# Merging the small TensorE products of two units in a Mamba block on Trainium2

## The chip, the cores and the metric

The kernel runs on one core of one Trainium2 chip. What is measured is the device time of one launch in microseconds (us). The core has five engines that run side by side and wait for each other through semaphores: TensorE (PE, with its weight loads shown apart as PEld), VectorE (DVE), ScalarE (ACT), GpSimd (POOL) and SyncE (SP, which here issues nearly all transfers).

## The reference

The block has four sequences of 512 tokens with 512 features. A conditioning vector gives six modulation vectors. The input is normalised, scaled and shifted, sent through a Mamba-2 layer, gated and added back; then it is normalised again, sent through a linear layer with a binarised weight, gated and added back. Cut to the Mamba layer, which is what the change touches:

```python
xBCzA = einsum('bld,ed->ble', h, in_proj_w)          # x, B, C, z and one step size per head
xBC   = silu(conv1d_4(xBC) + bias)                   # x: 64 heads of 16; B, C: 8 groups of 64
dt    = softplus(A_log)                              # (b, l, 64)
A_cum = cumsum(-dt) inside chunks of 128 tokens
Y_diag = (C . B) * exp(segsum(A)) applied to x       # inside a chunk
states = B^T . (x * exp(A_cum[-1] - A_cum))          # what a chunk leaves behind
new_states: states carried from chunk to chunk, decayed by exp(A_cum[-1])
Y_off  = (C . states) * exp(A_cum)                   # what earlier chunks add
out    = einsum((Y_diag + Y_off + D * x / dt) * silu(z + z_bias), out_proj_w)
```

All arrays are float32.

## The kernel before, in words

The 2048 tokens are eight halves `h` of 256 tokens, two to a sequence. Each half has two chunks `c` of 128 tokens, and the eight B/C groups are taken two at a time, as four pairs `gp`. A unit is one `(h, c, gp)`: 16 heads in one chunk. There are 64 units, and the loop at the end (lines 822 to 840) takes one unit a step. Feature rows stand on the 128 partitions, the two groups of a pair in the two halves of the partitions.

At step `s` of that loop the program first records the work of the next half (projections and convolutions for x, B, C and z in `conv_pair` and `f_z`, normalisation, step sizes in `f_dt`, transposes), spread over the steps by the lists `FRONT`, `FIRST` and `SECOND`, and the tails of finished chunks (output projection `tail1`, line 716; normalisation; linear layer `tail3`, line 753). Then it records the unit's own work:

- `burst(old, new)` (lines 593 to 607): the two products of unit `s` with the carried states (`gy<-C,S`, none in the first chunk of a sequence) and the two products B times C of unit `s+2` (`gy<-C,B`). Each product takes half of the partitions as its rows, so the two of a pair run side by side in the array (shown as `64*128`). They land in one PSUM tile `gy`, which has a single buffer of two banks and four slots of 128 columns; slots 0 and 1 are used.
- `stage2` of unit `s` (lines 627 to 694): 16 products `py` in two groups of eight (`128*32`, four side by side); DVE adds them to the state part (lines 663, 668) and POOL adds the skip and multiplies with the gate (669, 672). For the state that the chunk leaves, POOL makes `xd` (line 679, two buffers), PE the two products `pst` (line 684, `128*64`, side by side), and DVE copies them (687) or adds them to the decayed old state that POOL has made (689, 694). The states of a chunk are one tile `S` of four pairs.
- `stage0` and `stage1` of unit `s+2`: the loads of the running sums, the exponentials on ACT (line 544, 16 for a unit), the masked `gm` out of `gy` (618), and two large multiplications on DVE (622). `gm` and the unit's `yt` share three buffers.

`f_dt` (line 353) forms the product of the step sizes, `pa`, with eight matmuls of 64 columns (line 366), over k and, inside, over the two chunks; their right side is `hT`, which ACT writes one k at a time (line 347).

`glued` (line 208) keeps a list of matmuls together: the later ones are tied to the first and get a high priority. Lines 210 and 213 are its own, so `gy` and `py` show these two lines. Otherwise the order on each engine is set by a scheduler that takes the recorded instructions and their dependencies; matmuls that are not glued may be parted by others, as those of `pa` and `pst` are in some places. [...] The accumulators of the projections and the `pa` and `pst` tiles share five PSUM buffers (`mm`).

Of the kernel before, what the change touches and what calls it, by code (L numbers as in the profile page):

```python
# [11 lines left out]
F32 = mybir.dt.float32  # L12
# [4 lines left out]
P = 128  # L17
# [22 lines left out]
def adaln_mamba_block(  # L40
# [18 lines left out]
    def bc(ap, n):  # L59

        return ap.unsqueeze(2).to_broadcast([ap.shape[0], ap.shape[1], n])

    def bc_mid(ap, n):

        return ap.unsqueeze(1).to_broadcast([ap.shape[0], n, ap.shape[1]])
# [287 lines left out]
    def f_dt(h):  # L353

        hT = H[h]["hT"]

        def small(tag, bufs=1):  # L360
            return wk.tile([P, CH], F32, tag=tag, name=f"{tag}_{h}", bufs=bufs)

        pa = ps.tile([P, CH], F32, tag="mm", name=f"pa_{h}")
        for k in range(NK):
            for c in range(2):
                mm(pa[c * NH : (c + 1) * NH, :], win[:, k, NCONV + DI :],
                   hT[:, k, KS - 1 + c * CH : KS - 1 + (c + 1) * CH], start=(k == 0), stop=(k == NK - 1))
        u, r, q, dt, relu = (small(n) for n in ("du", "dr", "dq", "da", "dl"))
        nc.vector.tensor_scalar(relu, pa, 0.0, None, ALU.max)
        nc.scalar.activation(u, pa, AF.Abs)  # L370
        nc.scalar.activation(u, u, AF.Exp, scale=-1.0)
        nc.vector.tensor_scalar(r, u, 2.0, None, ALU.add)
        nc.vector.reciprocal(r, r)
        nc.vector.tensor_mul(u, u, r)
        nc.vector.tensor_mul(q, u, u)
        nc.vector.tensor_scalar(dt, q, SERIES[0], None, ALU.mult)
        for cf in SERIES[1:]:
            nc.vector.scalar_tensor_tensor(dt, dt, cf, q, ALU.add, ALU.mult)
        nc.vector.scalar_tensor_tensor(dt, dt, 1.0, u, ALU.add, ALU.mult)
# [12 lines left out]

        ntot = wk.tile([P, 1], F32, tag="ntot", name=f"ntot_{h}", bufs=1)
        nc.vector.tensor_scalar(ntot, up[:, CH - 1 : CH], -1.0, None, ALU.mult)
        ed = u
        nc.scalar.activation(ed, up, AF.Exp, bias=ntot)

        dg = q
        nc.vector.tensor_scalar(dg, ident, es[:, CH - 1 : CH], None, ALU.mult)

        nc.vector.reciprocal(r, dt)
        nc.vector.tensor_scalar(r, r, dsk, None, ALU.mult)
        with tc.issue_after(last_win):
            for c in range(2):
                nc.sync.dma_start(r_d[h, :, c, :], r[c * NH : (c + 1) * NH, :])
        H[h].update(turn=(sh, ed, dg))
# [185 lines left out]

    def burst(old, new):

        gy = ps.tile([P, 2, 4, CH], F32, tag="gy", bufs=1, name="gy_" + "_".join(map(str, old or new)))
        products = []
        if old is not None:
            h, c, gp = old
            k = (h % HPB) * 2 + c
            if k > 0:  # L600
                products += by_rows(gy, 1, h, c, gp, states[h // HPB, k][:, gp, :])
                G[old, 1] = gy
        if new is not None:
            h, c, gp = new
            products += by_rows(gy, 0, h, c, gp, H[h]["B"][gp // 2][:, gp % 2, c * CH : (c + 1) * CH])
            G[new, 0] = gy
        glued(products)

    def stage1(h, c, gp):

        n = f"{h}_{c}_{gp}"
        ets, e = U0.pop((h, c, gp))
        gm = wk.tile([P, 2, CH], F32, tag="gm", name=f"gm_{n}", bufs=3)
        nc.vector.tensor_mul(gm, G.pop(((h, c, gp), 0))[:, :, 0, :], bc_mid(upto, 2))  # L618
        if (h, c, gp) not in AHEAD:
            exps(h, c, gp, ets)  # L620
        for r in range(2):
            nc.vector.scalar_tensor_tensor(  # L622
                ets[r], ets[r], 1.0, bc_mid(gm[:, r, :], HPG), ALU.min, ALU.mult
            )
        U1[h, c, gp] = (ets, e)

    def stage2(h, c, gp):

        n = f"{h}_{c}_{gp}"
        k = (h % HPB) * 2 + c
# [12 lines left out]
        for r in range(2):  # L646
            glued([
                partial(
                    mm, py[32 * j : 32 * j + 32, r, :],
                    xp[:, r * 2 * P + 32 * (2 * j + q) : r * 2 * P + 32 * (2 * j + q) + 32],  # L650
                    ets[r][:, 2 * j + q, :], start=(q == 0), stop=(q == 1),
                )
                for q in range(2) for j in range(HPG // 2)
            ])

        cs = slice(c * CH, (c + 1) * CH)
        zg = H[h]["z"][gp][:, :, cs]
        xs = H[h]["xs"][gp][:, :, cs]
        t = wk.tile([P, 2, CH], F32, tag="gm", name=f"yt_{n}", bufs=3)

        ew = nc.vector if h == NHALF - 1 and c == 1 and gp >= NP // 2 else nc.gpsimd
        if k > 0:
            nc.vector.tensor_mul(t, G.pop(((h, c, gp), 1))[:, :, 1, :], e)
            if ew is nc.vector:
                ew.tensor_add(t, t, xs)
                ew.tensor_add(t, py, t)
            else:
                nc.vector.tensor_add(t, py, t)  # L668
                ew.tensor_add(t, t, xs)  # L669
        else:  # L670
            nc.vector.tensor_add(t, py, xs)  # L671
        ew.tensor_mul(zg, t, zg)  # L672

        if k < HPB * 2 - 1:
            if gp == 0:
                states[b, k + 1] = wk.tile([P, NP, P], F32, tag="S", name=f"S_{b}_{k + 1}")
            new = states[b, k + 1][:, gp, :]
            xd = wk.tile([P, HPG, 2, HD], F32, tag="xd", name=f"xd_{n}")
            nc.gpsimd.tensor_tensor(xd, xg, by_head(H[h]["ed"][:, hd0 : hd0 + HPP]), ALU.mult)  # L679
            xd2 = xd.rearrange("p j q e -> p (j q e)")  # L680
            pst = ps.tile([P, P], F32, tag="mm", name=f"pst_{n}")
            bt = H[h]["bt"][gp // 2][:, c, gp % 2, :]
            for r in range(2):
                mm(pst[r * NS : (r + 1) * NS, :], bt[:, r * NS : (r + 1) * NS], xd2[:, r * P : (r + 1) * P],  # L684
                   start=True, stop=True)
            if k == 0:
                nc.vector.tensor_copy(new, pst)
            else:
                nc.gpsimd.tensor_tensor(
                    new.rearrange("p (h e) -> p h e", e=HD),  # L690
                    states[b, k][:, gp, :].rearrange("p (h e) -> p h e", e=HD),
                    bc(H[h]["dec"][:, c * NP + gp, :], HD), ALU.mult,
                )
                nc.vector.tensor_add(new, new, pst)


    gates = {}
# [124 lines left out]
    for step in range(-1, max(steps) + 1):  # L822
        for f, args in steps.get(step, []):
            f(*args)

        new = units[step + 2 : step + 3] if step >= 0 else units[0:2]
        if step < 0:
            for unit in new:
                burst(None, unit)
                stage0(*unit)  # L830
                stage1(*unit)
        elif step < len(units):
            if new or not is_first(*units[step][:2]):
                burst(units[step], new[0] if new else None)
            stage2(*units[step])
            for unit in POST.get(step, []):
                ahead(*unit)
            for unit in new:
                stage0(*unit)
                stage1(*unit)  # L840
# [42 lines left out]
```

## Time and profile before

| | |
|---|---|
| median of 3 runs | 755.07 us (753.83 to 756.47) |
| the profiled execution | 755.08 us, of which the span of instructions is 753.4 us |
| mean granted TensorE clock | 0.984 |
| busy: PE, PEld | 713.0 us (95%), 505.6 us (67%) |
| busy: DVE, ACT, POOL | 610.8 us (81%), 520.1 us (69%), 258.5 us (34%) |
| instructions of line 684 (`pst`) and 366 (`pa`) as recorded passes | 192 and 128 |
| passes of `gy`: with B, with S | 256 and 192 |

A float32 matmul shows as two records (passes) in the trace, so that four records are one pair of products lying side by side. "Busy" of PE is modelled from start times; the start times themselves are recorded, and the time of a group of matmuls is best read from its own start to the start of the next group. Idle time of an engine that does not set the pace costs nothing.

### The profile page before, as it was taken

Reading aid. Unit: us, or ns where it says so; the run is one execution under the profiler, and the core shown is the slowest. Engines: PE = TensorE matmul, PEld = TensorE weight load, DVE = VectorE, ACT = ScalarE, POOL = GpSimd, SP = SyncE. Lnnn points to the kernel's source line nnn. Section 1 sums busy time; section 2 is a strip of 40 time slices with the busy share of each in tenths; the row PEclk is TensorE's granted clock in tenths of the full one; section 3 lists DMA queues with packets and bytes.
Section 4 is the critical chain, followed back from the end, with each engine's and each line's share of the span. In section 5 each row is a group of like instructions: output and inputs, shape, how many; then the busy total and the mean of one; then the engine's idle time right before and its main releaser. Section 6 shows DMA issues by size and latency. Waiting matters only on the chain. (4 is left out here: it accounts for less than half of the span.)

```text
span 753.4 us, 15095 instructions
## 1 busy us (share of the span) xinstructions
PE 713.0 (95%) x5196; PEld 505.6 (67%) x5196; DVE 610.8 (81%) x1226; ACT 520.1 (69%) x1503; POOL 258.5 (34%) x293
## 2 busy tenths in 40 slices
PE   6999868999999999999999999999999999999977
PEld 3786646766678666767677666786666766776643
DVE  3869888876998689976999669986898849996983
ACT  2486557749696587776777596875868758798920
POOL 4022345443143322343242341353213332334540
PEclk9999979999999999999999999999999999999989
DMA  8991583636553363424563355343634337455710
GB/s 282 313 291 42 188 193 96 166 80 144 117 142 105 84 173 105 130 68 112 142 154 105 75 142 136 113 127 90 163 89 111 93 84 182 123 161 124 161 35 28
DMA packets 121308, 99.25 MB, mean 132 GB/s; under 512 B 73984, under 2 KB 99840, under 8 KB 121232
## 3 DMA queue, kind: packets, MB, share of 16 engines
q1 hardware_dynamic: 120944, 97.76, 49.8%
q8 instruction: 41, 0.67, 0.4%
q10 hardware_dynamic: 288, 0.52, 0.2%
q14 instruction: 35, 0.29, 0.1%
HBM read 92.47 MB, written 5.79 MB: 130 GB/s over the span
## 5 line engine op out<-in xcount | busy, mean ns | idle before, releaser
L544 ACT ACTIVATE decay<-decay,st 128x128 f32<-128x128 f32 x960 | 293.3, 396 | 13.5 <-DMA decay<-sums_d 13.2
L622 DVE SCALAR_TENSOR_TENSOR decay<-decay,gm 128x1024 f32<-128x1024 f32 x120 | 155.3, 1295 | 28.3 <-ACT decay L544 26.4
L432 PE MATMUL pp_x<-hT,win 128*128 128x259 f32 x512 | 119.7, 388 | 0.0
L432 PE MATMUL pp_z<-hT,win 128*128 128x256 f32 x512 | 118.1, 383 | 0.0
L716 PE MATMUL po<-wout,z 128*128 128x512 f32 x256 | 114.2, 598 | 0.0
L679 POOL TENSOR_TENSOR xd<-xpad,st 128x256 f32<-128x256 f32 x48 | 35.0, 729 | 212.5 <-PE pst L684 161.1
L432 PEld LDWEIGHTS pp_x<-hT,win 128*128 128x128 f32 x512 | 96.2, 192 | 17.3 <-issue 2.6
L432 PEld LDWEIGHTS pp_z<-hT,win 128*128 128x128 f32 x512 | 94.3, 189 | 16.1 <-issue 3.0
L669 POOL TENSOR_TENSOR yt<-yt,xs 128x256 f32<-128x256 f32 x46 | 43.7, 950 | 128.5 <-DVE yt L668 115.9
L716 PEld LDWEIGHTS po<-wout,z 128*128 128x128 f32 x256 | 47.9, 191 | 53.8 <-issue 53.2
L449 DVE SCALAR_TENSOR_TENSOR u_x<-pp_x,cw,u_x 128x256 f32<-128x256 f32 x192 | 82.7, 474 | 0.8 <-ACT u_x L445 0.3
L213 PE MATMUL py<-decay,xpad 128*32 128x128 f32 x1680 | 68.8, 280 | 0.0
L511 ACT ACTIVATE uz<-pp_z,zb 128x256 f32<-128x256 f32 x64 | 26.8, 468 | 58.3 <-PE pp_z L432 58.3
L432 PE MATMUL pp_B<-hT,win 128*128 128x259 f32 x256 | 62.2, 395 | 0.8 <-DVE u_x L449 0.7
L672 POOL TENSOR_TENSOR z<-yt,z 128x256 f32<-128x256 f32 x62 | 57.2, 922 | 11.6 <-DVE yt L671 8.2
L502 POOL TENSOR_TENSOR xs<-u_x,rr 128x512 f32<-128x512 f32 x32 | 44.1, 1378 | 46.4 <-DVE u_x L454 38.4
L753 PE MATMUL pf<-bwT,h 128*128 128x512 f32 (+1 forms) x136 | 59.3, 576 | 0.6 <-ACT h L737 0.6
L432 PE MATMUL pp_C<-hT,win 128*128 128x259 f32 x256 | 59.5, 385 | 0.0
L445 ACT ACTIVATE u_x<-pp_x,cb,cw 128x256 f32<-128x256 f32 x64 | 35.1, 559 | 33.1 <-PE pp_x L432 32.9
L210 PE MATMUL py<-decay,xpad 128*32 128x128 f32 x240 | 48.0, 282 | 8.5 <-ACT decay L544 6.8
L432 PEld LDWEIGHTS pp_B<-hT,win 128*128 128x128 f32 x256 | 48.1, 194 | 11.2 <-DVE u_x L449 1.5
L432 PEld LDWEIGHTS pp_C<-hT,win 128*128 128x128 f32 x256 | 48.4, 192 | 7.8 <-issue 0.5
(155 smaller groups left out, 1144.5 us busy)
## 6 DMA issues: line engine op xcount, KB each, us to landing
decay<-sums_d SPq DMA_DIRECT2D x120, 256.0 KB
decay<-sums_d SPq DMA_DIRECT2D x120, 128.0 KB
rr<-r_d SPq DMA_DIRECT2D x64, 128.0 KB
e<-e_d SPq DMA_DIRECT2D x96, 64.0 KB
win<-in_w_inT SPq DMA_DIRECT2D x4, 1024.0 KB
xr<-in_x SPq DMA_DIRECT2D x16, 256.0 KB
res<-o SPq DMA_DIRECT2D x15, 256.0 KB
x<-in_x SPq DMA_DIRECT2D x14, 256.0 KB
```

What stands on the lines that cost most here:

```text
L210: first = products[0]()
L213: product()
L432: last = mm(pm, win[:, k, col : col + P], H[h]["hT"][:, k, lo:], start=(k == 0), stop=(k == NK - 1))
L445: nc.scalar.activation(u[:, j, :], pm[:, KS - 1 :], AF.Identity, bias=cb[:, t : t + 1], scale=cw[:, t, KS - 1 : KS])
L449: nc.vector.scalar_tensor_tensor(u[:, j, :], pm[:, k : k + T], cw[:, t, k : k + 1], u[:, j, :], ALU.mult, ALU.add)
L502: nc.gpsimd.tensor_tensor(xs, xc, rr, ALU.mult)
L544: nc.scalar.activation(ets[r][:, i, :], ets[r][:, i, :], AF.Exp, bias=H[h]["st"][:, hd : hd + 1], scale=-1.0)
L622: nc.vector.scalar_tensor_tensor(ets[r], ets[r], 1.0, bc_mid(gm[:, r, :], HPG), ALU.min, ALU.mult)
L669: ew.tensor_add(t, t, xs)
L672: ew.tensor_mul(zg, t, zg)
L716: last_po = mm(po, H[h]["z"][g // 2][:, g % 2, c * CH : (c + 1) * CH], wout[:, g, :], start=(g == 0), stop=(g == NKI - 1))
L753: mm(pf, h2[:, k, :], bwT[:, k, cols], start=(k == 0), stop=(k == NK - 1))
```

## The change

Three things are done in larger pieces. A burst now serves two units at once: at every even step it forms the state products of units `s` and `s+1` and the B times C products of units `s+2` and `s+3`, in all four slots of `gy`; at odd steps there is none. The new states of two neighbouring pairs are formed together at the odd step, by a new function: four glued products into one PSUM tile, and one copy, or one multiplication and one addition, of 256 columns. The product of the step sizes is glued, and takes k downwards in every half but the first.

```diff
@@ f_dt
-        for k in range(NK):
-            for c in range(2):
-                mm(pa[c * NH : (c + 1) * NH, :], win[:, k, NCONV + DI :],
-                   hT[:, k, KS - 1 + c * CH : KS - 1 + (c + 1) * CH], start=(k == 0), stop=(k == NK - 1))
+        ks = range(NK) if h == 0 else range(NK - 1, -1, -1)
+        glued([
+            partial(
+                mm, pa[c * NH : (c + 1) * NH, :], win[:, k, NCONV + DI :],
+                hT[:, k, KS - 1 + c * CH : KS - 1 + (c + 1) * CH], start=(k == ks[0]), stop=(k == ks[-1]),
+            )
+            for k in ks for c in range(2)
+        ])
@@ burst
-        if old is not None:
-            h, c, gp = old
+        for i, (h, c, gp) in enumerate(old):
             k = (h % HPB) * 2 + c
             if k > 0:
-                products += by_rows(gy, 1, h, c, gp, states[h // HPB, k][:, gp, :])
-                G[old, 1] = gy
-        if new is not None:
-            h, c, gp = new
-            products += by_rows(gy, 0, h, c, gp, H[h]["B"][gp // 2][:, gp % 2, c * CH : (c + 1) * CH])
-            G[new, 0] = gy
+                products += by_rows(gy, 2 + i, h, c, gp, states[h // HPB, k][:, gp, :])
+                G[(h, c, gp), 1] = gy[:, :, 2 + i, :]
+        for i, (h, c, gp) in enumerate(new):
+            products += by_rows(gy, i, h, c, gp, H[h]["B"][gp // 2][:, gp % 2, c * CH : (c + 1) * CH])
+            G[(h, c, gp), 0] = gy[:, :, i, :]
         glued(products)
@@ stage2
-            if gp == 0:
-                states[b, k + 1] = wk.tile([P, NP, P], F32, tag="S", name=f"S_{b}_{k + 1}")
-            new = states[b, k + 1][:, gp, :]
             xd = wk.tile([P, HPG, 2, HD], F32, tag="xd", name=f"xd_{n}")
             nc.gpsimd.tensor_tensor(xd, xg, by_head(H[h]["ed"][:, hd0 : hd0 + HPP]), ALU.mult)
-            ...
+            XD[gp % 2] = xd.rearrange("p j q e -> p (j q e)")
+            if gp % 2:
+                new_states(h, c, gp - 1)
+
+    XD = {}
+
+    def new_states(h, c, gp):
+        k = (h % HPB) * 2 + c
+        b = h // HPB
+        if gp == 0:
+            states[b, k + 1] = wk.tile([P, NP, P], F32, tag="S", name=f"S_{b}_{k + 1}")
+        both = slice(gp, gp + 2)
+        new = states[b, k + 1][:, both, :].rearrange("p g e -> p (g e)")
+        pst = ps.tile([P, 2, P], F32, tag="mm", name=f"pst_{h}_{c}_{gp}")
+        bt = H[h]["bt"][gp // 2]
+        glued([
+            partial(
+                mm, pst[r * NS : (r + 1) * NS, i, :], bt[:, c, i, r * NS : (r + 1) * NS],
+                XD[i][:, r * P : (r + 1) * P], start=True, stop=True,
+            )
+            for i in (1, 0) for r in range(2)
+        ])
+        pst = pst.rearrange("p g e -> p (g e)")
+        if k == 0:
+            nc.vector.tensor_copy(new, pst)
+        else:
+            nc.gpsimd.tensor_tensor(
+                new.rearrange("p (h e) -> p h e", e=HD),
+                states[b, k][:, both, :].rearrange("p g (h e) -> p (g h) e", e=HD),
+                bc(H[h]["dec"][:, c * NP + gp : c * NP + gp + 2, :].rearrange("p j h -> p (j h)"), HD), ALU.mult,
+            )
+            nc.vector.tensor_add(new, new, pst)
@@ the loop over steps
         if step < 0:
+            burst([], new)
             for unit in new:
-                burst(None, unit)
                 stage0(*unit)
                 stage1(*unit)
         elif step < len(units):
-            if new or not is_first(*units[step][:2]):
-                burst(units[step], new[0] if new else None)
+            if step % 2 == 0 and (step + 2 < len(units) or not is_first(*units[step][:2])):
+                burst(units[step : step + 2], units[step + 2 : step + 4])
             stage2(*units[step])
```

More of the change, by code (lines that the diff above doesn't have):

```diff
@@ L593, in burst @@
     def burst(old, new):
-        gy = ps.tile([P, 2, 4, CH], F32, tag="gy", bufs=1, name="gy_" + "_".join(map(str, old or new)))
+        gy = ps.tile([P, 2, 4, CH], F32, tag="gy", bufs=1, name="gy_" + "_".join(map(str, (old or new)[0])))
         products = []
-        if old is not None:
-            h, c, gp = old
+        for i, (h, c, gp) in enumerate(old):
             k = (h % HPB) * 2 + c
             if k > 0:
-                products += by_rows(gy, 1, h, c, gp, states[h // HPB, k][:, gp, :])
-                G[old, 1] = gy
-        if new is not None:
-            h, c, gp = new
-            products += by_rows(gy, 0, h, c, gp, H[h]["B"][gp // 2][:, gp % 2, c * CH : (c + 1) * CH])
-            G[new, 0] = gy
+                products += by_rows(gy, 2 + i, h, c, gp, states[h // HPB, k][:, gp, :])
[3 more added lines that the diff above has]
+            G[(h, c, gp), 0] = gy[:, :, i, :]
         glued(products)
@@ L617, in stage1 @@
         gm = wk.tile([P, 2, CH], F32, tag="gm", name=f"gm_{n}", bufs=3)
-        nc.vector.tensor_mul(gm, G.pop(((h, c, gp), 0))[:, :, 0, :], bc_mid(upto, 2))
+        nc.vector.tensor_mul(gm, G.pop(((h, c, gp), 0)), bc_mid(upto, 2))
         if (h, c, gp) not in AHEAD:
@@ L662, in stage2 @@
         if k > 0:
-            nc.vector.tensor_mul(t, G.pop(((h, c, gp), 1))[:, :, 1, :], e)
+            nc.vector.tensor_mul(t, G.pop(((h, c, gp), 1)), e)
             if ew is nc.vector:
@@ L674, in stage2 @@
         if k < HPB * 2 - 1:
-            if gp == 0:
-                states[b, k + 1] = wk.tile([P, NP, P], F32, tag="S", name=f"S_{b}_{k + 1}")
-            new = states[b, k + 1][:, gp, :]
             xd = wk.tile([P, HPG, 2, HD], F32, tag="xd", name=f"xd_{n}")
             nc.gpsimd.tensor_tensor(xd, xg, by_head(H[h]["ed"][:, hd0 : hd0 + HPP]), ALU.mult)
-            xd2 = xd.rearrange("p j q e -> p (j q e)")
-            pst = ps.tile([P, P], F32, tag="mm", name=f"pst_{n}")
-            bt = H[h]["bt"][gp // 2][:, c, gp % 2, :]
@@ L683, in stage2 @@
[L683 to L694, printed above, removed]
+            XD[gp % 2] = xd.rearrange("p j q e -> p (j q e)")
```

## The prediction

> **What bounds the kernel now.** I read the busy table and slices first, then PE's own waits, then one step of PE's timeline, then stages.
>
> ```profile
> PE 713.0 (95%) x5196; PEld 505.6 (67%) x5196; DVE 610.8 (81%) x1226; ACT 520.1 (69%) x1503; POOL 258.5 (34%) x293
> PE   6999868999999999999999999999999999999977
> DVE  3869888876998689976999669986898849996983
> ```
>
> PE is at 9 from the eighth slice (132 us) to the end of the 38th (716 us), DVE is not. So PE sets the pace, except at both ends. PE's waits agree: nearly all of them are a few single places.
>
> ```profile
> PE pbw L285 <- DVE u_C L449: 7.2, 1, 7.2
> PE py L210 <- ACT decay L544: 6.8, 6, 2.4
> PE pa L366 <- ACT hT L347: 3.8, 4, 1.2
> PE gy L210 <- DVE gm L618: 0.2, 1, 0.2
> ```
>
> (Who waits for whom: total us, times, longest.) So what PE saves counts, wherever no other engine is as late. What can it save without doing less? The timeline of PE shows it: start, duration, records.
>
> ```profile
> 312.78 0.39 PE L213 MATMUL gy<-C,B 64*128 64x128 f32 x4
> 313.10 0.30 PE L210 MATMUL py<-decay,xpad 128*32 128x128 f32 x1
> 314.11 0.44 PE L684 MATMUL pst<-xd,bt 128*64 128x128 f32 x4
> 314.48 3.77 PE L432 MATMUL pp_x<-hT,win 128*128 128x259 f32 x16
> ```
>
> The burst begins at 312.46, so start to start it takes 0.64 for 8 records, py 1.01 for 32, pst 0.37 for 4. Bursts of 4 records take 0.42, py groups of 16 take 0.58, pa groups of 4 and 8 take 0.37 and 0.59. Four more records (one more pair of products) thus cost 0.22, sixteen of py 0.43; what is left over is a fixed part: 0.42 - 0.22 = **0.20 us** for a burst, 0.37 - 0.22 = **0.15** for a stretch of pst or pa, 0.58 - 0.43 = **0.15** for py. It is paid each time the shape of the array (64*128, 128*32, 128*64, 128*128) changes, and it is the same to 0.01 us through the run.
>
> **The change part by part.** I count stretches of one shape in the order in which PE's instructions stand in the two programs. Before: 66 bursts, 74 stretches of py, 72 stretches of 64 columns (pst, pa and the small sums, which share their shape). After: 33, 69, 34. The products are as many as before, so only fixed parts go.
> - Bursts: 33 x 0.20 = 6.6 us.
> - 64 columns: 24 of the 38 are single pst pairs that join others, the rest is pa, which other matmuls had cut up: 38 x 0.15 = 5.7 us.
> - py: 5 x 0.15 = 0.75 us.
>
> Together 13.0 us of PE time. The other engines: 48 DVE pieces on pst (32 of 272 ns, 16 of 278 ns: 13.2 us) become 24 of 256 columns; the nearest row is an addition of that shape from PSUM:
>
> ```profile
> L668 DVE TENSOR_TENSOR yt<-py,yt 128x256 f32<-128x256 f32 x46 | 19.0, 414 | 0.9 <-PE py L213 0.8
> L694 DVE TENSOR_TENSOR S<-S,pst 128x128 f32<-128x128 f32 x32 | 8.7, 272 | 0.0
> L689 POOL TENSOR_TENSOR S<-S,st 128x128 f32<-128x128 f32 x32 | 24.5, 775 | 34.6 <-PE gy L213 16.6 <-DVE S L687 11.8 <-DVE S L694 6.2
> ```
>
> 24 x 0.414 = 9.9 us, so DVE loses 3.2 us of work; POOL's 32 multiplications become 16 of twice the width, between 0.73 us (its xd of 256 columns) and 1.55 (twice 775 ns), so 0 to 13 us less; I take 8. Both engines idle for over 140 us; I count neither by itself. No DMA is added or dropped. SP's list is nearly the same: the e loads of some units and, in half 1, the writes of the step sizes move by one or two places, past loads of decay tiles. Those writes then stand behind loads that wait for the py of unit 3; their readers come over 10 us later, so I cost them at nothing; uncovered, they would hold SP some 5 us once.
>
> How much of the 13.0 reaches the end? Four places take from it.
>
> *The opening, 60 to 107 us.* Here PE waits for DVE:
>
> ```profile
> 60.00:80.00 20.00, 18.46 (x178) 11.98 (x176) 17.43 (x36) 11.44 (x30) 6.47 (x8) 1.00 0.18 46
> 80.00:100.00 20.00, 12.79 (x93) 10.09 (x92) 19.03 (x45) 10.46 (x31) 7.94 (x7) 0.89 0.60 194
> ```
>
> (Stage, length, busy PE, PEld, DVE, ACT, POOL, granted clock, DMA share, GB/s.) About 1.0 us of the fixed parts lie here and are worth nothing. But pa of half 1, which before ran in three pieces between projections (77.35 to 80.0), now runs in one (about 1.0 us from 77.35), and DVE, which idled 1.65 us for it just then, starts its step-size chain 1.7 us earlier; in the new order it also does one of the big multiplications ahead. Against a wait of 7.2 us on DVE I credit 1.5. Net: 0.5 gained. The skill's "TensorE: Matmul & The Clock Gate" (What's actually happening) says that the clock halves after an idle window of about 3.4 us and stays so for about as long. The row here is milder: after 7.2 us of idling, 16 records of pp_x took 5.18 us where they take 3.67 to 3.77 elsewhere. By the rule, a stall cut below 3.4 us would save that 1.4 us too; by the row the stall only falls to some 5 us, and I take nothing.
>
> *The passage from one half to the next.* PE waits 0.92 us for the decays in the odd halves and 1.16 for hT in the even ones, so ACT paces it. pa now begins with the hT that ACT writes last. At 270 us ACT finishes hT at 272.05; eight matmuls of pa (0.15 + 4 x 0.22 = 1.0) and the four of pst in the same shape (0.43) then end at 273.5, where before the last pst ended at 273.33: no gain though 0.5 was counted. In the even ones (hT at 184.2, end before 186.40, after 185.65) the count holds. Lost: 3 x 0.65 = 2.0 us.
>
> *Other waits on ACT.* Three of the six waits of py for decays lie outside those passages (0.8 to 2.4 us, near 213, 389 and 566 us), and one of 2.0 us before the transposes ph at 125 us. They stay ACT's; where PE comes earlier they grow. I take 0.4 us for each of the four, 1.6 us (between 0, if ACT comes earlier too because PE feeds it, and some 4).
>
> *The end.* From 660 us ACT is busy 19.2, 18.1 and 18.1 us of each 20, and DVE 19.5 in the last:
>
> ```profile
> 700.00:720.00 20.00, 19.77 (x204) 12.13 (x201) 19.52 (x27) 18.14 (x59) 10.05 (x9) 1.00 0.69 142
> ```
>
> There lie about 5 bursts and 3 pst, 1.4 us, which I write off; one burst less after 729 us, where PE waits for nobody, gives 0.4 back. Lost: 1.0.
>
> Sum: 13.0 + 0.5 - 1.0 (opening) - 2.0 - 1.6 - 1.0 = 7.9, and 0.9 more for DVE's and POOL's lighter work in stages where DVE is at 9 (0.3 of the 3.2 us): **8.8 us**. Span 753.4 - 8.8 = 744.6; around it lie 755.08 - 753.4 = 1.7 us: **746.3 us**. The profiled time equals the median, so this is set against 755.07.
>
> One rule speaks against the larger burst. "PSUM — Partial Sum Buffer" (PSUM bank collisions raise a hardware error) wants PSUM guarded by bank, not by address: gy has one buffer of two banks, so the next burst may not write before DVE has taken all four parts, two gm and two yt, where it was two parts before. By the rule every burst could wait for DVE; the row is PE's wait above, 0.2 us in all, and the last reader (gm of unit s+3) is recorded one step, about 11 us, before the next burst, as now. By the row the sum stays; by the rule it would lose whatever DVE lags. The first reader gets its data later, by two pairs (0.44 us), on an engine with slack.
>
> **The rivals.**
> - *All 13 us arrive*, because ACT and DVE are themselves fed by PE (ACT waited 58.3 us for pp_z and 32.9 for pp_x) and move up with it; the clock recovers too: 755.1 - 13 - 1 = 741.
> - *ACT and DVE become the bound.* In slices where DVE stands at 9, PE is only about 1 us in 20 ahead of it. If half of the remaining gain is lost: 755.1 - 4 = 751.
> - *Nothing happens* (the fixed part is only hidden fill): 755. Against it: groups of 4 and 8 differ by 0.22, not by half of 0.64.
> - *Slower: bursts that wait.* gm and yt share three buffers, so gm of unit s+3 needs POOL to have finished the gate of unit s; a late POOL holds gm, gm holds the single gy, and PE stands with the projections queued behind the burst. Of 33 bursts 31 have a predecessor in the loop. Each wait of 0.28 us eats the gain (8.8 / 31); from (8.8 + 2.3) / 31 = 0.36 us the kernel is over 0.3% slower; at 0.4 us it takes 755.1 - 8.8 + 12.4 = 758.7. For it: one buffer, and DVE waited for POOL's z before gm. Against: that wait was 0.3 us in all.
>
> **How the numbers follow.** Full gain 0.16, the likeliest (743 to 749.5) 0.60, ACT and DVE as bound 0.12, nothing 0.05, slower 0.07. About 0.3% (2.3 us) is what a measurement of this kernel can tell from no change. Below 752.8: the first three, 0.88 less a little of the third: 0.87. Within: 0.06. Slower: 0.07. The range of 8 in 10 reaches from the full gain to past the third case: 740.5 to 752.
>
> **What would show it.** Right: PE's line with about 700 us busy, 33 bursts, 8-record pst of 0.59 us and bursts of 16 records of about 1.07, projections unchanged at 3.7. Wrong: py waiting for ACT decay by more than 10 us in all, pa for hT by more than 6, gy for gm or yt by more than 2, or the 7.2 us wait of pbw grown, since a DVE order that puts the weight signs later would cost more than all passages together.

## The result and the profile after

The changed kernel takes **765.69 us** (median of three executions, 764.35 to 767.69; 754.45 before in the same series). The ratio to the kernel before is 1.0149, with a 95% interval of 1.0109 to 1.0188: 11 to 12 us slower, where 8.8 us faster was forecast. A fourth execution, at a granted clock of 0.557 throughout (1195.5 us), is left out, and the profile below is of the same kernel in the next series (median 766.4 us): a span of 765.1 us at a mean granted clock of 0.979.

The page of the changed kernel, busy table and slices:

```profile
PE 703.9 (92%) x5196; PEld 506.6 (66%) x5196; DVE 617.5 (81%) x1202; ACT 520.0 (68%) x1503; POOL 247.8 (32%) x277
PE   6998868999989989999989989899998998999977
DVE  3969899876989689977898859987699858987883
```

PE's own time fell from 713.0 to 703.9 us, although 4 us more of the span's clock were withheld (0.979 of 765.1 us granted against 0.984 of 753.4). But PE's row, which was an unbroken line of 9 before, now has an 8 in most halves. The span is 765.1 us, so PE stands still for 61.2 us, where it stood for 40.4. PE's waits in the changed kernel (total us, times, longest):

```profile
PE pbw L285 <- POOL sw L278: 6.9, 2, 5.1
...
PE py L210 <- DVE decay L625: 5.9, 6, 1.4
PE pp_B L437 <- ACT decay L549: 5.1, 3, 1.7
PE ph L753 <- DVE t L300: 5.1, 3, 2.4
PE pst L210 <- ACT st L430: 5.1, 3, 2.0
PE pt_bt L467 <- DVE u_x L454: 4.6, 4, 1.4
PE py L210 <- ACT decay L549: 4.5, 6, 1.2
...
PE pa L210 <- ACT hT L347: 1.6, 4, 0.4
...
PE gy L210 <- DVE gm L621: 1.3, 1, 1.3
```

All of PE's waits come to 57.1 us, against 36.3 before: 20.8 more, less 9.1 of busy time, gives the 11.7 by which the spans differ. The new ones (`pp_B`, `pst`, `pt_bt`) are small and recur in every half: PE wants a PSUM tile that ACT or DVE has not yet emptied. PE's timeline in half 3 shows one, and the merged pieces (start, duration, records):

```profile
307.24 0.29 PE L210 MATMUL pst<-xd,bt 128*64 128x128 f32 x1 [1.82 <-ACT st L430]
...
307.83 3.77 PE L437 MATMUL pp_B<-hT,win 128*128 128x259 f32 x16
...
319.35 0.37 PE L210 MATMUL gy<-C,S 64*128 64x128 f32 x1
...
320.44 0.30 PE L210 MATMUL py<-decay,xpad 128*32 128x128 f32 x1
```

Start to start, `pst` of 8 records takes 0.59 us and a burst of 16 records 1.09: the prices of the prediction (0.59 and 1.07). `pst` had stood still for 1.82 us first.

### The profile page after: what moved, and what is told of

The parts are those of the page before. It is cut to its first block, busy times and chain, and to the rows that moved or that the text cites. A ratio compares the mean times of both kernels' runs of the same rounds, so it can differ in the third digit from the quotient of the medians.

```text
span 1193.8 us, 15005 instructions
## 1 busy us (share of the span) xinstructions
PE 1172.8 (98%) x5196; PEld 619.2 (52%) x5196; DVE 622.4 (52%) x1202; ACT 526.2 (44%) x1503; POOL 243.9 (20%) x277
## 4 chain that ended last, share of the span: by engine, by line
PE 98%; DVE 1%; POOL 1%; DMA 0%; issue 0%; ACT 0%; ACTq 0%; DVEq 0%; POOLq 0%
PE pp_x L437 17%; PE pp_z L437 17%; PE po L734 17%; PE pp_B L437 8%; PE pp_C L437 8%; PE pf L771 8%; PE py L213 5%; PE py L210 4%; PE gy L213 3%; PE pt_xt L467 2%; PE gy L210 1%; PE pt_bt L467 1%; PE ph L753 1%; PE phT L330 1%; PE pst L210 1%; PE pa L213 1%
## 5 line engine op out<-in xcount | busy, mean ns | idle before, releaser
L437 PE MATMUL pp_x<-hT,win 128*128 128x259 f32 x512 | 204.4, 584 | 0.5 <-DVE u_C L454 0.5
L437 PE MATMUL pp_z<-hT,win 128*128 128x256 f32 x512 | 204.2, 584 | 0.0
L734 PE MATMUL po<-wout,z 128*128 128x512 f32 x256 | 200.6, 968 | 0.0
L437 PEld LDWEIGHTS pp_x<-hT,win 128*128 128x128 f32 x512 | 114.3, 227 | 79.1 <-issue 49.4
L437 PEld LDWEIGHTS pp_z<-hT,win 128*128 128x128 f32 x512 | 112.2, 223 | 79.2 <-issue 51.2
L771 PE MATMUL pf<-bwT,h 128*128 128x512 f32 (+1 forms) x136 | 101.9, 921 | 0.6 <-ACT h L755 0.6
L437 PE MATMUL pp_B<-hT,win 128*128 128x259 f32 x256 | 102.4, 583 | 0.0
L437 PE MATMUL pp_C<-hT,win 128*128 128x259 f32 x256 | 102.4, 584 | 0.0
L213 PE MATMUL py<-decay,xpad 128*32 128x128 f32 x1680 | 101.9, 377 | 0.0
L437 PEld LDWEIGHTS pp_C<-hT,win 128*128 128x128 f32 x256 | 57.5, 227 | 40.1 <-issue 25.5
L213 PEld LDWEIGHTS py<-decay,xpad 128*32 128x32 f32 x1680 | 60.7, 127 | 7.2
```

The costliest lines, as they stand in the source:

```text
L213: product()
L437: last = mm(pm, win[:, k, col : col + P], H[h]["hT"][:, k, lo:], start=(k == 0), stop=(k == NK - 1))
L734: last_po = mm(po, H[h]["z"][g // 2][:, g % 2, c * CH : (c + 1) * CH], wout[:, g, :], start=(g == 0), stop=(g == NKI - 1))
L771: mm(pf, h2[:, k, :], bwT[:, k, cols], start=(k == 0), stop=(k == NK - 1))
```

## The experiments

All times are medians; the kernel before took 754.8 to 755.4 us beside them, and each ratio is to its own neighbour. "Standing" is the span of the one profiled execution less PE's busy time in it (40.4 us before). "Old order" is explained further down.

| run | us | ratio to before | PE busy | standing |
|---|---|---|---|---|
| whole change | 766.4 | 1.0148 (1.0120 to 1.0176) | 703.9 | 61.2 |
| bursts alone | 758.0 | 1.0043 (1.0028 to 1.0058) | 707.9 | 50.7 |
| states alone | 753.0 | 0.9980 (0.9967 to 0.9992) | 705.8 | 44.5 |
| step sizes alone | 765.7 | 1.0142 (1.0110 to 1.0175) | 710.9 | 52.1 |
| step sizes, old order | 758.3 | 1.0054 (1.0037 to 1.0071) | 712.7 | 44.1 |
| whole change, old order | 751.7 | 0.9964 (0.9949 to 0.9980) | 701.2 | 48.0 |
| bursts, old order | 756.1 | 1.0010 (0.9996 to 1.0024) | 705.7 | 46.6 |
| step sizes glued, k upwards | 758.4 | 1.0055 (1.0037 to 1.0072) | 716.4 | 40.3 |
| whole change, only PE in old order | 780.2 | 1.0325 (1.0302 to 1.0347) | 712.2 | 68.0 |
| whole change, only DVE in old order | 771.6 | 1.0214 (1.0189 to 1.0240) | 702.5 | 63.1 |
| whole change, only ACT in old order | 753.5 | 0.9968 (0.9952 to 0.9984) | 700.1 | 49.4 |
| bursts and states, old order | 749.7 | 0.9918 (0.9893 to 0.9943) | 702.3 | 47.0 |
| whole change, one ACT step back | 772.7 | 1.0263 (1.0202 to 1.0324) | 703.6 | 66.1 |
| before, that ACT step ahead | 755.6 | 1.0005 (0.9994 to 1.0016) | 712.1 | 42.3 |
| step sizes, only ACT in old order | 757.2 | 1.0043 (1.0025 to 1.0061) | 714.1 | 45.9 |
| bursts and states, own order | 758.4 | 1.0045 (1.0030 to 1.0060) | 701.8 | 53.7 |
| before, more DVE work | 757.3 | 1.0024 (1.0011 to 1.0038) | 712.9 | 43.5 |
| whole change, less DVE work | 761.9 | 1.0086 (1.0059 to 1.0113) | 695.9 | 60.8 |

### Which part costs

The whole change once more, and each of its three parts alone, with the other two as in the kernel before:

```diff
 # bursts alone
-                burst(units[step], new[0] if new else None)
+                burst(units[step : step + 2], units[step + 2 : step + 4])
 # states alone
+            if gp % 2:
+                new_states(h, c, gp - 1)
 # step sizes alone
+        ks = range(NK) if h == 0 else range(NK - 1, -1, -1)
+        glued([
...
```

> The changed kernel again, for a trace at the full TensorE clock; nothing is changed in it. All theories expect some 765 us, as in the timed runs. Theory W (bursts wait): the trace shows PE waiting for DVE or POOL ahead of gy, 15 to 25 us in all. Theory H (step sizes late): PE waits ahead of pa for hT, 7 to 15 us in all. Theory O (the opening): the stall before the transposes of the weight signs, 7.2 us before, has grown by 8 us or more, with the clock low after it, and the later halves are each 1 to 2 us shorter than before.

> Only the bursts are made in pairs; the new states and pa stay as before. By the fixed parts 7.6 us of PE time go. Theory W: about 10 us slower than before (the whole loss and more lies here). Theories H and O without W: 4 to 7 us faster.

> Only the new states are made in pairs. By the fixed parts 4.2 us of PE time go. Theory W and H: 2 to 4 us faster. Theory O, if the order of DVE and POOL in the opening is what hurts: 5 us or more slower.

> Only pa is glued and takes k downwards. By the fixed parts 2.4 us of PE time go. Theory H: 5 to 10 us slower, a wait of about 1.2 us ahead of pa in each of seven halves. Theory W: within 2 us of before. Theory O: within 2 us, or slower with a longer stall in the opening.

Bursts +3.2 us, states -1.9, step sizes +10.9: together +12.2, close to the +11.6 of the whole. So the step sizes' product, the part with the fewest instructions, costs most by itself. (The parts do not add up in general: bursts and states together, measured further down, take 3.3 us more and not 1.3.) But the product isn't late by itself: PE waits for `hT` ahead of it less than before (1.6 us in the whole change and 0.3 with this part alone, 3.8 before). The bursts wait for `gm` once, 1.3 us, and half 2 begins 1.8 us later than before. None of the three mechanisms that I had in mind (W, H and O) is large enough to be the cause.

A look at the orders of the programs gave the next idea. Counting k downwards, the product begins with the `hT` that ACT writes last; the scheduler arranges the other engines' instructions anew around it. By the traces, with the product glued and k upwards DVE's order is that of the kernel before except in 6 of 1226 rows, and ACT's is the same; with k downwards 205 rows of DVE and 193 of ACT's 1503 stand elsewhere. How many rows move does not tell the loss: with the bursts alone it is 270 and 179, for 3.2 us.

### The same work in the old order

To part the work from its order, every instruction of an engine is tied behind its forerunner, in an order written out (`ORDER`: the old one, two pieces that became one standing where the second stood, a burst where the even step's stood). The ties are of a kind without a wait (`NoSync`); they only leave the scheduler no choice. The traces show the lists kept: with the step sizes' part in the old order, all 1226 rows of DVE and 1503 of ACT stand as in the kernel before. In the whole change POOL is left to the scheduler.

```diff
+def in_order(tc, traced):
+    by_name = {i.name: i for i in traced}
+    for engine in ORDER:
+        names = ["I-" + n for n in ORDER[engine].split()]
+        for earlier, later in zip(names, names[1:]):
+            tc.add_manual_dep(
+                by_name[later], earlier,
+                mybir.DependencyInfo(mybir.DependencyClass.NoSync, mybir.DependencyReason.DATA), reason="order",
+            )
...
         adaln_mamba_block(tc, *aps, res)
+        in_order(tc, list(nc.cur_bb.bb.instructions))
```

The fourth run of this series leaves the orders to the scheduler and glues the product with k upwards:

```diff
-        ks = range(NK) if h == 0 else range(NK - 1, -1, -1)
+        ks = range(NK)
```

> The step sizes' product as changed (one piece, k downwards), but every instruction of DVE, ACT, POOL and SP is tied to the place that it has in the kernel before, and PE's too, except for the product itself and the three or four neighbours that it stands between. Theory R (the change of k lets the scheduler put the work of the other engines in a worse order, and that costs the 11 us): 752 to 755, as 14 stretches less on PE are worth 2.1 us at most. Theory P (the product is late because it begins with the hT that ACT writes last, whatever the others do): 763 to 767, as in the run of this part alone (765.7).

> The whole change, with the orders of DVE, ACT and SP of the kernel before (two pieces that became one stand where the second stood), PE in its old order with the merged pieces in place, POOL left to the scheduler. 33 bursts, 34 stretches of 64 columns, 68 of py: 13.2 us of fixed parts less than before. Theory R: 745 to 750, the prediction's sum. Theory D (DVE and ACT set the pace in most stretches, PE's saved time is not on the path): 753 to 756. Theory P: 763 or more.

> The burst for two units alone, all five engines in the order of the kernel before, each burst at the place of the even step's. 33 bursts instead of 66 and 3 stretches less: 7.0 us of fixed parts. Theory R: 748 to 752 (in its own order this part alone took 758.0). Theory D: 754 to 756. Rival W of the bursts (they wait for all readers of the one buffer): 758 or more, and PE waits for gm or yt by over 5 us.

> The step sizes' product in the glued form but with k upwards in every half. DVE, ACT and SP keep the order of the kernel before (six DVE rows apart); on PE the product is cut into more pieces than before, by py: 9 more stretches of 64 columns and 12 more of py, 21 x 0.15 = 3.2 us more fixed parts. Theory R with fixed parts that count in full: 757 to 759. If fixed parts are hidden (theory D): 754 to 756. Gluing itself as the cause: 763 or more.

The whole change in the old order takes 751.7 us: 3.3 us faster than before, 14.7 faster than the same instructions in the scheduler's own order. So **the order costs more than the change saves**. Two of the parts show the same at their own size: the step sizes lose 3.3 us instead of 10.9, the bursts 1.0 instead of 3.2 (the states alone were not run in the old order). Ties as such do not make a kernel fast: two later runs of the whole change, tied throughout to its own order but for small edits, take 772.7 and 761.9 us.

The order is not all, though. None of the three came as early as I expected from the order alone (752 to 755, 745 to 750, 748 to 752). With the bursts in the old order PE's busy time falls by 7.3 us and the time not at all (ratio 1.0010, 0.9996 to 1.0024): what PE saves there, it stands longer. PE's busy time and waits of the whole change in the old order:

```profile
PE 701.2 (94%) x5196; PEld 505.6 (67%) x5196; DVE 611.8 (82%) x1202; ACT 520.5 (69%) x1503; POOL 247.2 (33%) x277
```

```profile
PE py L210 <- ACT decay L549: 10.5, 9, 1.7
PE pbw L285 <- DVE u_C L454: 6.3, 1, 6.3
...
PE py L210 <- DVE decay L625: 6.1, 7, 1.2
...
PE pp_B L437 <- DVE u_x L454: 0.8, 3, 0.3
```

`pst` and `pt_bt` no longer wait, `pp_B` hardly. What is left beyond the kernel before is mostly `py`, which waits 16.6 us for decays (7.9 before).

The glued product with k upwards, in which the other engines keep nearly their old order, measures the fixed part. By PE's order it has 9 stretches of 64 columns and 12 of `py` more than before, since `py` now cuts the product up further; by the prediction's prices that is 21 x 0.15 = 3.2 us. Time rose by 3.3 us, PE's busy time by 3.4. So added fixed parts arrive in full, where saved ones did not:

```profile
PE 716.4 (95%) x5196; PEld 505.4 (67%) x5196; DVE 610.8 (81%) x1226; ACT 520.4 (69%) x1503; POOL 258.8 (34%) x293
```

### Which engine's order, and pieces as filling

The same ties on one engine at a time in the whole change (`ORDER` with that engine's list alone), and bursts and states with the step sizes' product left as before, in pieces, in the old order (POOL left to the scheduler).

```diff
-ORDER = {"PE": ..., "DVE": ..., "Activation": ..., "SP": ...}
+ORDER = {"Activation": ...}
```

> The whole change, with PE alone tied to the order that it has in the run in the old order (751.7); DVE, ACT, POOL and SP as the scheduler then puts them. Theory A (PE's own order is what went wrong: it asks for tiles that DVE or ACT have not emptied yet): 751 to 754. Theory B (DVE's order) or C (ACT's order): 762 to 767, as the whole change (766.4). Theory M (the orders of several engines have to fit each other): between, 756 to 761.

> The whole change, with DVE alone tied to its old order (1167 rows the same; 38 of PE's and over 100 of ACT's still stand elsewhere). Theory B: 751 to 755. Theories A and C: 762 to 767. Theory M: 756 to 761.

> The whole change, with ACT alone tied to its old order. Theory C: 751 to 755. Theories A and B: 762 to 767. Theory M: 756 to 761.

> Bursts and states as changed, the step sizes' product as before (in pieces, k upwards), all in the old order with POOL left to the scheduler: 2.55 us more fixed parts than the whole change in the old order (751.7). Theory F (the pieces of the product fill PE while ACT and DVE finish the decays, and the whole piece waits where they filled; py waited 16.6 us for decays there, 7.9 before): 747 to 751, although PE has more to do. If the filling is worth nothing: 753 to 755.

With ACT alone in its old order the kernel takes 753.5 us, nearly all that the old order gives. With PE alone it is 780.2, with DVE alone 771.6, both worse than with none, which I had not expected of either. The scheduler arranges the free engines around the tied one, so these runs don't say that ACT's list is right by itself; they say that orders are worth something only in a set that fits, and that the set which the scheduler builds around ACT's old list fits.

Bursts and states with the product in pieces give **749.7 us**, the fastest of all, 0.8% below the kernel before, although PE has 2.55 us more of fixed parts than in the whole change. A likely reason is that the pieces fill PE while ACT and DVE finish the decays: over the first 10 us from the transposes of `hT`, summed over halves 2 to 6, PE's timeline shows 5.3 us of waits before, 8.9 with the product in one piece (whole change, old order; 8.4 with the step sizes' part alone), 6.1 with the pieces. That this is the whole reason is not shown. From 30 to 40 us into these halves the run with the pieces waits longer (7.9 us against 5.7), and the two profiled executions are equally long (749.3 and 749.2 us); the 2.0 us between the two kernels stand in the medians, of 4 and 15 executions.

### One suspected instruction, ACT's part alone, and the pair in its own order

In the changed kernel ACT has `du<-pa` (0.28 us, the absolute value of the step sizes' product) ahead of the eight exponentials of the next unit in halves 2 to 7, and idles 12.7 us for it (4.1 before). This instruction is moved behind them in the changed kernel (in halves 3, 5 and 7 with its exponential, which stood beside it), and ahead of them in the kernel before; everything else stays tied to the order that each of the two kernels has by itself.

```diff
 # "Activation" list, half 4, changed kernel
 hT hT hT hT
-du<-pa
 decay0 x8
+du<-pa
 du<-du
```

The third run ties ACT alone in the step sizes' part; the fourth is bursts and states without any ties.

> The whole change with every engine tied to its own order as changed, but for one instruction of ACT in each of halves 2 to 7: the absolute value of the step sizes' product (with the exponential of it, where that stood beside it) moves from before the eight exponentials of the next unit to behind them. Theory S (this one place makes the decays late, about 2 us in each half): 754 to 758. If it is one of several places: 759 to 763. If ACT's idle time there costs nothing: 765 to 768.

> The kernel before, every engine tied to its own order, but for the absolute value of the step sizes' product, which ACT now takes ahead of the eight exponentials in halves 2 to 7. Theory S: 762 to 768 (six times some 2 us). If this place costs only together with the changed orders of DVE and PE: 755 to 758.

> The step sizes' part alone (765.7 in its own order, 758.3 in the old one), with ACT alone tied to its old order. There the absolute value already stands behind the exponentials; other places of ACT differ (an evacuation of x ahead of the next unit's exponentials, and two of B and C further on). If ACT's order is what costs in this part too: 756 to 760. If here it is DVE's or PE's: 763 to 767.

> Bursts and states as changed, the step sizes' product as before, every engine as the scheduler puts it. In the old order this took 749.7. By the sum of the two parts alone (+3.2 and -1.9 us): 756. If the scheduler's order suits the pair: 750 to 753. If it breaks down again as in the whole change: 762 or more.

The suspicion falls both ways. In the kernel before, ACT now idles 14.0 us for `du` and the time is the same (755.6). In the changed kernel the move costs 6 us more (772.7). DVE's and PE's waits of that run, 0.6 and 4.6 us without the move:

```profile
DVE dr L377 <- ACT du L376: 10.9, 4, 3.7
```

```profile
PE pt_bt L467 <- DVE u_x L454: 12.9, 5, 3.6
```

DVE stands at `dr`, the next link of the step sizes' chain, which its list has early, with the emptying of `pp_x` into `u_x` queued behind it, and PE stands at `pt_bt` until DVE has written `u_x`. With ACT tied, the step sizes' part takes 757.2 instead of 765.7, as in the fully old order (758.3). And the pair that took 749.7 in the old order takes 758.4 in the scheduler's: once more about 9 us that only the order makes. By the two parts alone (+3.2 and -1.9) it would have been 756.

### Whether DVE has slack where PE waits

Where does the order bite? In the whole change mostly in one place. From 30 to 40 us after the start of a half (the transposes of `hT`), PE's timeline has 4.5 us of waits in halves 2 to 6 before, 5.7 in the whole change in the old order, 14.9 in its own: 9.2 of the 13.2 us by which all of PE's waits differ between the two orders. The step sizes' part alone is not explained by it: there this place has 5.2 us in its own order and 4.4 in the old one, and the 8.2 us by which its waits differ are spread (3.4 from 60 to 70 us, the rest mostly at both ends). In half 4 of the changed kernel (PE):

```profile
393.89 0.63 PE L467 MATMUL pt_bt<-ident,B 128*128 128x128 f32 x4 [1.43 <-DVE u_x L454]
...
397.98 5.42 PE L437 MATMUL pp_B<-hT,win 128*128 128x259 f32 x16 [1.71 <-ACT decay L549]
```

DVE in the same place:

```profile
390.11 0.16 DVE L297 TENSOR_SCALAR rs_f<-mv_f 128x1 f32<-128x1 f32 x1
390.17 0.49 DVE L454 SCALAR_TENSOR_TENSOR u_x<-pp_x,cw,u_x 128x256 f32<-128x256 f32 x1
392.02 0.55 DVE L300 TENSOR_SCALAR t<-xr,mv_f,rs_f 128x512 f32<-128x512 f32 x1 [1.37 <-POOL rs_f L298]
392.49 2.44 DVE L454 SCALAR_TENSOR_TENSOR u_x<-pp_x,cw,u_x 128x256 f32<-128x256 f32 x6
```

and in the old order (whole change):

```profile
380.63 0.44 DVE L454 SCALAR_TENSOR_TENSOR u_x<-pp_x,cw,u_x 128x256 f32<-128x256 f32 x1
381.00 0.14 DVE L297 TENSOR_SCALAR rs_f<-mv_f 128x1 f32<-128x1 f32 x1
381.06 0.47 DVE L454 SCALAR_TENSOR_TENSOR u_x<-pp_x,cw,u_x 128x256 f32<-128x256 f32 x1
381.92 0.55 DVE L300 TENSOR_SCALAR t<-xr,mv_f,rs_f 128x512 f32<-128x512 f32 x1 [0.39 <-POOL rs_f L298]
382.38 1.65 DVE L454 SCALAR_TENSOR_TENSOR u_x<-pp_x,cw,u_x 128x256 f32<-128x256 f32 x4
```

The half begins at 362.98 and at 354.42. In the changed order PE's `pt_bt` starts 0.1 us after the fourth of the reads that empty `pp_x`. That read is done 30.8 us into the half in the changed order (the third of the last six) and 28.8 in the old one (the second of the last four), while PE is free for `pt_bt` after about 29.4 in both (end of the `pn` matmuls). Half of these 1.9 us is the normalisation `t`, for which DVE stands 1.0 us longer; the rest it brings along. The stretch from 5 to 35 us of halves 3 and 4, before and then changed (start and end, length, busy PE, PEld, DVE, ACT, POOL, clock, DMA share, GB/s):

```profile
273.10:303.10 30.00, 29.75 (x197) 21.41 (x195) 27.68 (x67) 22.14 (x66) 7.31 (x10) 1.00 0.61 156
361.40:391.40 30.00, 29.18 (x209) 21.31 (x208) 29.20 (x69) 21.82 (x65) 8.96 (x9) 1.00 0.56 135
```

```profile
277.30:307.30 30.00, 27.24 (x196) 19.79 (x193) 27.41 (x62) 21.37 (x65) 5.49 (x8) 1.00 0.58 136
368.00:398.00 30.00, 26.86 (x187) 19.25 (x183) 26.29 (x65) 21.07 (x64) 4.69 (x6) 1.00 0.51 111
```

Before, DVE is busy for 29.2 of 30 us in half 4, as PE is; in the changed order for 26.3, and it waits for the rest. In half 3 DVE's time differs little. Over halves 2 to 6 it is busy for 141.3 of 150 us before and 132.6 in the changed order. Its waits for the exponentials grew with it, from 26.4 us in 35 places to 40.1 in 39, over the whole kernel:

```profile
DVE decay L622 <- ACT decay L544: 26.4, 35, 1.8
```

```profile
DVE decay L625 <- ACT decay L549: 40.1, 39, 2.8
```

The last two runs put a price on this: 0.94 us more DVE work in each of seven halves of the kernel before, and 1.1 us less in the changed one, all orders tied to each kernel's own.

```diff
 # before, more DVE work
+        if h > 0:
+            nc.vector.reciprocal(dt, r)
         nc.vector.reciprocal(r, r)
 # whole change, less DVE work
-        nc.vector.tensor_scalar(dt, q, SERIES[0], None, ALU.mult)
-        for cf in SERIES[1:]:
+        terms = SERIES if h == 0 else SERIES[4:]
+        nc.vector.tensor_scalar(dt, q, terms[0], None, ALU.mult)
+        for cf in terms[1:]:
```

> The kernel before, every engine tied to its own order, with one more DVE instruction in each of halves 1 to 7: a reciprocal of 128x128 (0.94 us by the same instruction in the profile) ahead of the reciprocal of the step sizes' chain, its result overwritten by the next but one. Theory D2 (DVE is as late as PE in the first 30 us of a half, already before the change): 7 x 0.94 = 6.6 us in full, 759 to 762. If DVE has half a microsecond of slack there: 757 to 758. If PE alone sets the pace, as the prediction had it: 754 to 756.

> The whole change, every engine tied to the changed kernel's own order, with the step sizes' series cut to its last five coefficients in halves 1 to 7: four DVE instructions of 0.28 us less in each, 1.1 us. Theory D2: PE gets its PSUM tiles earlier by as much, 7 x 1.1 = 7.7 us: 757 to 761. If DVE only waits longer for ACT or POOL instead: 764 to 767.

The added instruction in the kernel before:

```profile
L374 DVE RECIPROCAL da<-dr 128x128 f32<-128x128 f32 x7 | 6.6, 941 | 0.0
```

Of 6.6 us put in, 2.2 arrive at the end (0.8 to 2.9 by the interval): the kernel before had an estimated 0.6 us of slack on DVE in each half (4.4 / 7). Of 7.7 us taken out of the changed kernel, 4.5 come back, but not as expected. PE's waits from 30 to 40 us fall only from 14.9 to 12.2 us, and all its waits from 57.1 to 56.6; `pt_bt` now waits for ACT there, no longer for DVE:

```profile
PE pt_bt L468 <- ACT decay L550: 2.5, 2, 1.2
```

The granted clock of that run is higher: executions of 0.984 to 0.989, where the changed kernel has 0.979 to 0.984. At 0.984, which both have, the spans are 761.1 and 763.5 us against 763.2 and 764.2: by these few executions some 1.4 us for the work itself, the rest for the clock (more on it at the end). So DVE's work by itself explains little of the loss. DVE is close behind PE before the change, and after it stands waiting for ACT and POOL with the emptying of PE's tiles behind; by these executions most of the work taken out turns into waits for others.

## Why the prediction was wrong

**The step that failed is the sum itself**: "The products are as many as before, so only fixed parts go", followed by "Four places take from it". It takes the order of the other engines in the steady halves as given. I compared orders for counts of PE's stretches, for SP's transfers and for the opening, and not what DVE and ACT do in each half. The missing term is what the new order costs: 14.7 us (766.4 against 751.7 for the same instructions). A second, smaller error is in "How much of the 13.0 reaches the end?": with the old order held, 3.3 us arrive and not 8.8, as ACT and DVE were closer behind PE than the sum allows. The two together, 14.7 and 5.5 us, are the distance between the forecast and the result.

Point by point:

- *The fixed parts* (13.0 us): right as PE's own time, to some 3 us. PE's busy time fell by 11.8 us in the old order at the same granted clock (0.984), for 13.2 us counted; by 10.7 for 10.65 with the pieces; by 7.3 for 7.0 with the bursts; it rose by 3.4 for 3.2 with the product cut up. (These last three had a clock of 0.986, about 1.5 us less withheld.) In their own orders the bursts alone gave 5.1 for 7.6 and the states alone 7.2 for 4.2, these at 0.988.
- *The other engines' pieces*: right as prices (the merged states take 413 ns on DVE, where 414 was used, and 863 ns on POOL, inside the bounds), what they are worth in time no run parts. DVE's busy total even rose, from 610.8 to 617.5 us (611.8 in the old order); why is open.
- *The opening*: forecast 0.5 us to the good; from the start of half 1 to that of half 2 it takes 107.6 us instead of 107.0. `pbw` waits 6.9 us instead of 7.2 and 1.3, but `pp_x` now waits 2.3 us for `u_C`. The stall for the most part moved. The sum takes the 1.0 us of this stage off twice ("Net: 0.5 gained" has it already): by its own terms it gives 9.8 and not 8.8, further from the result.
- *The passages*: 2.0 us lost was the right place, at too small a size and with half of the mechanism. In the old order the waits in the first 10 us grew by 3.6 us in five halves, and by 3.1 with the step sizes' part alone, which lost 3.3. I had asked when `pa` ends, and not what PE does in the gap that its pieces filled.
- *Bank rule and bursts*: as the row said and not as the rule: `gy` waited for `gm` once, 1.3 us. The slower rival did not decide either.
- *The end*: forecast 1.0 us lost; half 7, the last, takes 133.1 us instead of 130.9.
- *ACT and DVE as bound* (rival, 751): with the old order held, this is where the kernel lands (751.7). The sentence behind it, that PE is only about 1 us in 20 ahead of DVE, fits the 0.6 us of slack in each half and the bursts that gain nothing in the old order; it should have carried more weight than 0.12. That the number fits to 1 us is in part luck, since the rival puts it at half of what remained without a reason.
- *Signs*: the signs of being right all came (33 bursts, 0.59, 1.09, about 700 us), and none of the signs of being wrong (`py` for ACT 4.5, `pa` 1.6, `gy` 1.3, `pbw` no longer). A list of waits that were there before can't show a wait that wasn't.

What stays open is which instructions of the new order are at fault. Tying ACT's list undoes it, moving the instruction that looked guilty doesn't, and PE's or DVE's list alone makes it worse; a smaller set than ACT's whole list was not found. Nor is it shown where the loss of the step sizes' part comes from when it stands alone, beyond that its order makes 7.4 us of it.

## What to carry to other kernels

Where a scheduler sets the orders, compare every engine's order over one steady period before adding up what a change saves, and run the change once with the old order tied: that parts what the work costs from what its place costs, and here the second (14.7 us) was more than four times the first (3.3). Ask of a second engine how many tenths of a microsecond it has left in the stage, by a window of that stage, since a row of tenths shows 9 for both. Small pieces that look wasteful may be what fills the bounding engine while others finish: look first whether they lie in a busy stretch or in a gap.

## What the hardware showed

The granted clock makes a small wait dear, and not each time. After the waits of 1.43 and 1.71 us above, `pp_B` took 5.42 us for 16 records that take 3.77 elsewhere, 1.65 us more. Waits of about the same sum at this place in halves 2, 3, 5 and 6 brought no such loss. The windows (stretch, length, busy PE, PEld, DVE, ACT, POOL, clock, DMA share, GB/s) show when the clock fell:

```profile
394.84:398.25 3.41, 1.70 (x33) 1.09 (x22) 3.41 (x8) 3.23 (x11) 0.00 (x0) 1.00 0.43 112
398.25:401.67 3.42, 3.42 (x9) 2.69 (x8) 3.42 (x7) 3.42 (x11) 0.84 (x1) 0.50 0.55 132
```

The wait of 1.71 us lies whole in the first of these stretches, half of which PE is thus idle; for the next 3.41 us the clock is halved, so 1.7 us are withheld. In each of the 19 traces that this text draws on, the starts of the halved stretches lie whole multiples of 3.41 us apart. Cut along this grid from 20 us on, the traces have 3930 pieces at full clock. Of 3815 with up to 1.65 us of PE idle, by the profile's busy time, none is followed by a halved one; of 67 with 1.97 us or more, all are; of 48 between, 16. So in these traces the halving follows a piece of the grid in which PE is idle for about half or more, and how the grid happens to lie decides whether a wait falls whole into one piece.

"TensorE: Matmul & The Clock Gate" (What's actually happening) in the Trainium skill says of a window of about 3.4 us that it runs free of the kernel, which agrees with the grid. Its table has the clock fall after an idle window of that length, and so did the prediction; here a window half idle was enough, and the longest wait in it was 1.71 us.

Such losses are also most of the spread of the kernel before with one ACT step ahead: its spans lie at 756.3 us for a clock of 0.982, 754.7 to 755.1 for 0.984, 752.9 to 754.6 for 0.986 and 752.1 to 753.8 for 0.989. In other kernels the groups overlap more (the whole change in the old order has 749.1 us at 0.983 and 750.6 at 0.989). In the profiled execution of the changed kernel there are four such losses from 120 to 650 us and two before, which makes 2 x 1.7 = 3.4 us of the 11.
